# Two more y buffers and a longer lookahead in the second stage of a four-layer convolution kernel

## The chip, the cores and the metric

The kernel runs on one core of one Trainium2 chip. The metric is the time on the device in microseconds (us), the median of three runs. The profile is that of one further execution of the same program.

## What is computed

The input is `x` of shape [8192, 8, 16, 16] in float32: 8192 samples of 8 channels and 16 x 16 points. Four layers follow each other, each of the form x + f(gn(x)), where `gn` is a normalization over the two channels of each of four groups:

```python
x = x + L0(gn(x))   # a tensor-train operator with three cores of rank 8, plus a bias
x = x + L1(gn(x))   # 3x3 convolution, then batch norm over all samples, then relu
x = x + L2(gn(x))   # input and weights quantized to +-127 by their maxima, 3x3 convolution
x = x + L3(gn(x))   # weights binarized to sign * mean, 3x3 convolution with edge padding
```

with, for the two layers that cut the kernel into stages,

```python
# L1: the mean and variance go over all 8192 samples
mean = y.mean(axis=(0, 2, 3), keepdims=True)
var = y.var(axis=(0, 2, 3), keepdims=True)
return relu(gamma * (y - mean) * rsqrt(var + EPS) + beta)
# L2: the scale needs the largest value of the whole normalized input
sx = MAX_Q / jnp.max(jnp.abs(x))
```

The mean and variance of layer 1 need all samples before one can be finished, and so does the maximum of layer 2. That is why the kernel goes over the data three times.

## The kernel before, in words

**Tiles.** The samples are cut into `NT` = 64 tiles of 128. A tile has 128 partitions (8 channels x 16 rows) and 2,048 float32 values in each (128 samples x 16 columns), 1 MiB in all. Tiles that don't fit into SBUF between the stages are kept in DRAM: `x1_d` (the sum after layer 0), `y_d` (the convolution of layer 1), `x2_d` (the centred sum after layer 1).

**Stage 1** (lines 328 to 685) works in quarters of a tile, 256 steps. It computes layer 0 on TensorE, adds it to x, normalizes, computes the convolution of layer 1 and its statistics. Each x1 and y goes to DRAM, except for the last `STAY` = 4 tiles, which remain in SBUF. Layer 0 needs its operand in another arrangement: `limbs` (line 401, its stores are line 409) writes a high and a low part of it to `limb_d` in DRAM by 8 small transfers on SyncE's queue (SP), and `fetch` (line 411) reads it back into one of two `xl` buffers by a transfer that GpSimd issues, 252 in all. The descriptors of such a transfer are written by GpSimd into a reserve in SBUF. The buffers `sq0` and `sq1` serve for squares there, `xh` for the high parts of the limbs; TensorE's expanded operands lie in `u`.

**Constants** (lines 688 to 708): mean and variance of layer 1 become the pair `bn_a`, `bn_b`.

**Stage 2** (lines 743 to 871) is the one that the change touches. It goes over the tiles in `order2`: the four that stayed first, then 0 to 59. In the following, "tile i" is the i-th in this order. Its steps for one tile are

- `sum2`: ScalarE applies relu(bn_a y + bn_b) to the y buffer, GpSimd adds it to the x buffer, so that the y buffer is free from here on,
- `square2` (ScalarE), `sums2` (TensorE, sums of groups), `stats2` and `sigma2` (VectorE, ScalarE and a pow on GpSimd: mean and 1/deviation),
- `spread2`: VectorE builds `diag_b` from them and transposes it, TensorE spreads it to all partitions (`gb`, `gr`),
- `centre2`: VectorE subtracts the mean from x in two halves, and SP stores x to `x2_d` (line 827). The last 13 tiles before the last five (`KEEP` = 13, `LATE` = 5) are not stored but kept for stage 3,
- `range2`: VectorE takes maxima for the scale of layer 2 into `top`.

The loop (line 853) runs over i and calls in turn: the loads, `sum2(i)`, `sums2(i-2)`, `spread2(i-3)`, `square2(i-1)`, `stats2(i-2)`, `centre2(i-3)`, `sigma2(i-2)`, `range2(i-3)`. Work on TensorE, VectorE, ScalarE and GpSimd is kept in this order (`InOrder`, lines 31 to 44; line 43 is what the profile shows for all of it). SP's transfers are ordered by the framework, which may put them in another order than the code's.

**Buffers of stage 2.** There are 13 x buffers (`x_slots`, line 95, and two `xk` of line 746) and 8 y buffers (`y_slots`, line 96: one of the tiles that stayed, `sq0`, `sq1`, `xh`; and four `yk` of line 747). `load2(i)` (line 104, its transfer is line 111) loads tile i's y into y buffer (i - 4 + 1) mod 8 and its x into x buffer i mod 13. So the x of tile j takes the place of tile j - 13, which must have been stored, and the y of tile j that of tile j - 8, whose `sum2` must be done.

```python
AHEAD2 = len(y_slots) - 1
```

`AHEAD2` (line 845), 7 here, is the lookahead: step i of the loop loads y, then x of tile i + 7, and the store of tile i - 3 comes later in that step. The first loads are earlier: those of tiles 4 to 6 stand in the code at the end of stage 1 (lines 663 to 677: y and x of 4 and 5 in the last but one step, x of 6 and 7, then y of 6), the y of 7 and both of 8 and 9 ahead of the loop, those of 10 at step 1. The last five tiles (`LATE`, lines 858 to 861) are loaded one transfer a step into y buffers that have become free.

**Stage 3** (from line 888 on) computes layers 2 and 3. The order of its steps is that of a table of due times (`PHASE`, `PERIOD`). It loads x from `x2_d` (line 911) into the same x buffers, uses `sq0`, `sq1`, `xh` and `y_stay[3]` as work space, and stores the output (line 1053).

Of the kernel before, what the change touches and what calls it, by code (L numbers as in the profile page):

```python
# [8 lines left out]
F32 = mybir.dt.float32  # L9
# [9 lines left out]
P = 128  # L19
C, H, W = 8, 16, 16  # L20
CH = C * H
F = P * W
G = 4
R = 8
NQ = 4
# [37 lines left out]
def tile_net(ctx: ExitStack, tc: tile.TileContext, xb, xt_in, pack0, pack1, pack2, out):  # L63
    nc = tc.nc
    NT = xt_in.shape[0]
# [10 lines left out]
    def load_pack(src, parts, t):  # L76
        nc.scalar.dma_start(t, src)
        views, at = {}, 0
        for key, n in parts:
# [3 lines left out]


    hold = ctx.enter_context(tc.tile_pool(name="hold", bufs=1))
    xs, bs, ys, sqs, (xh,) = ([hold.tile([P, F], F32, name=f"{n}{k}") for k in range(m)]
                            for n, m in (("xs", 4), ("bs", 2), ("ys", 2), ("sq", 2), ("xh", 1)))
    us = [hold.tile([P, 2 * F], F32, name=f"u{k}") for k in range(2)]

    STAY = 4  # L90
    order2 = list(range(NT - STAY, NT)) + list(range(NT - STAY))
    y_stay = [ys[NT % 2], ys[(NT - 1) % 2], bs[NT % 2], bs[(NT - 1) % 2]]
    y_of = dict(zip(order2, y_stay))

    x_slots = ([xs[t % 4] for t in order2[:STAY]] + [u[:, h * F:(h + 1) * F] for u in us for h in range(2)] + y_stay[:3])
    y_slots = [y_stay[3]] + sqs + [xh]
    T2 = [dict() for _ in range(NT)]

    LATE = 5 if NT >= KEEP + STAY + 3 else 0
# [4 lines left out]
    def load2(i, what="yx"):  # L104
        for k in what:
            if k == "x":
                T2[i]["x"] = x_slots[i % KEEP]
            else:
                T2[i]["y"] = y_stay[i] if i < STAY else y_slots[(i - STAY + 1) % len(y_slots)]
            if i >= STAY:  # L110
                nc.sync.dma_start(T2[i][k], (x1_d if k == "x" else y_d)[order2[i]])
# [216 lines left out]
    with first as s:  # L328
# [19 lines left out]
        def load_b(t):  # L348
            T[t]["xb"] = bs[t % 2]
            n = F // 2 if t == 0 else F  # L350
            for a in range(0, F, n):
                nc.sync.dma_start(T[t]["xb"][:, a:a + n], xb[t][:, a:a + n])
# [84 lines left out]
        def main(t, q, between, n0=None):  # L437
            u = T[t].pop(("u", q)).rearrange("p b (s n) -> p b s n", s=R)
            po = ps_m.tile([P, BANK], F32, name=f"po_{t}_{q}", tag="mm")
            parts = [(0, QS)] if n0 is None else [(0, n0), (n0, QS)]  # L440
            for a, b in parts:
                for r in range(R):
                    for f, args in between.get(r, ()) if b == QS else ():
                        f(*args)
                    pe.matmul(samples(po)[:, a:b], core01[:, r], u[:, a:b, r, :], start=(r == 0), stop=(r == R - 1))
            cols = slice(q * BANK, (q + 1) * BANK)
            x = T[t]["x"]
            dve.tensor_tensor(x[:, cols], po, x[:, cols], ALU.add)
# [66 lines left out]
        def conv1(t, q):  # L515
            v = T[t].pop(("v", q))
            pm, po = (ps_m.tile([P, k, NC], F32, name=f"{n}_{t}_{q}", tag="mm") for n, k in (("pm", 4), ("pc", 2)))
            for ps, at in ((pm, 0), (po, 4)):
                for k in range(ps.shape[1]):
                    pe.matmul(ps[:, k], L["fast1"][:, at + k], v[:, at + k], start=True, stop=True)  # L520
            m = wk.tile([P, 2, NC], F32, name=f"m_{t}_{q}", tag="m")
            act.activation(m[:, 0], pm[:, 0], AF.Identity, bias=L["b1"], scale=1.0)
            act.copy(m[:, 1], pm[:, 2])
            T[t]["m", q] = m, pm, po
# [40 lines left out]
        def quarter_of(n, lag):  # L565

            t, q = divmod(n - lag, NQ)
            return (t, q) if 0 <= t < NT else None
# [34 lines left out]
        for n in range(NT * NQ):  # L603
            t, q = divmod(n, NQ)
            steps = {}

            def at(r, ok, f, *args):
                if ok:
                    steps.setdefault(r, []).append((f, args))

            def at1(r, f, lag):
                if quarter_of(n, lag):
                    at(r, True, f, *quarter_of(n, lag))

            last, before, ahead = t == NT - 1, t > 0, t + 2 < NT
            if n > 0:
                next(rest, None)
                if n == 1:
                    next(rest, None)
            tn, qn = divmod(n + 1, NQ)  # L620
            at(0, tn < NT, expand, tn, qn, 0)
            at(4, tn < NT, expand, tn, qn, 1)
            at1(0, conv1_input, LAG)
            if n < NT * NQ - 1:
                at1(6, conv1_scaled, LAG - 1)
            if n == 0 and NT > 1:
                at(1, True, norm_b_spread, 1)
                at(1, True, norm_b_apply, 1)
                at(1, True, add_bias, 1)
            if q == 0:  # L630
                if before and t - 1 not in y_of:
                    nc.sync.dma_start(x1_d[t - 1], T[t - 1]["x"])
                at(1, before, norm_sums, t - 1)
                at(4, before, norm_stats, t - 1)
                if ahead:
                    load_b(t + 2)
            elif q == 1:
                at(1, ahead, norm_b_square, t + 2)
                at(1, before, norm_apply, t - 1)
                at(4, t + 3 < NT, load_t, t + 3)  # L640
            elif q == 2:
                at(1, ahead, norm_b_sums, t + 2)
                at(1, ahead, norm_b_stats, t + 2)
            else:
                at(1, before and t + 3 < NT, add_bias, t + 3)
                at(1, ahead, norm_b_spread, t + 2)
                at(1, ahead, norm_b_apply, t + 2)
            at1(3, conv1_output, LAG + 1)

            for m in {0: [], 1: [4, 5], 2: [6, 7], 3: []}.get(n, [n + NQ]):  # L650
                at(0 if n < 3 else 2, m < NT * NQ, limbs, *divmod(m, NQ))
            for m in {0: [], 1: [4, 5], 2: []}.get(n, [n + 3]):
                at(5, m < NT * NQ, fetch, *divmod(m, NQ))

            at(2, n == NQ and NT > 2, add_bias, 2)
            at(5, n == NQ + 1 and NT > 3, add_bias, 3)
            if last:
                at(2, q > 1, quarter_apply, t, q - 2)
                at(2, q > 0, quarter_stats, t, q - 1)
            main(t, q, steps, n0=QS // 2 if n == 0 else None)  # L660
            if quarter_of(n, LAG):
                conv1(*quarter_of(n, LAG))
            if n == NT * NQ - 2 and NT > STAY + 3:
                load2(STAY)
                load2(STAY + 1)

        t = NT - 1
        if NT > STAY + 3:
            load2(STAY + 2, "x")
            load2(STAY + 3, "x")  # L670
        conv1_output(t - 1, 1)
# [1 line left out]
        quarter_stats(t, 3)  # L673
        conv1_direct(t, 0)
        quarter_apply(t, 2)
        if NT > STAY + 3:
            load2(STAY + 2, "y")
        conv1_direct(t, 1)
        for q in (2, 3):
            conv1_direct(t - 1, q)  # L680
# [63 lines left out]
    with tc.tile_pool(name="p2", bufs=2) as p2, tc.tile_pool(name="ps2", bufs=2, space=PSUM) as ps2:  # L744
# [9 lines left out]
        for k in range(3):  # L754
            nc.tensor.matmul(kps, L["gpad"].rearrange("p q j -> p (q j)"), L["band3"][:, k],
                             start=(k == 0), stop=(k == 2))
        ksum = p2.tile([P, CH], F32, name="ksum", tag="ksum", bufs=1)
        nc.vector.tensor_tensor(ksum.rearrange("p (c h) -> p c h", c=C), kps.rearrange("p (c h) -> p c h", c=C),
                                L["mean3"].unsqueeze(2).to_broadcast([P, C, H]), ALU.mult)
        nc.vector.tensor_tensor(L["corr"], L["corr"], ksum, ALU.subtract)  # L760
# [79 lines left out]
        def on(i, f):  # L840
            if 0 <= i < NT:
                f(i)

        BEGUN = STAY + 3 if NT > STAY + 3 else STAY
        AHEAD2 = len(y_slots) - 1


        free = STAY + AHEAD2 - 1
        for i in [*range(STAY), *range(BEGUN, free)]:
            on(i, lambda i: load2(i, "y" if i == BEGUN > STAY else "yx"))  # L850
        y_used = {}
        late = [(k, j) for j in range(NT - LATE, NT) for k in "yx"]
        for i in range(NT + 4):
            if i == 1:
                on(free, load2)
            if i + AHEAD2 < NT - LATE:
                on(i + AHEAD2, lambda i: i <= free or load2(i))
            elif late:
                k, j = late.pop(0)
                T2[j][k] = y_used[i - 1]  # L860
                nc.sync.dma_start(T2[j][k], (x1_d if k == "x" else y_d)[order2[j]])
            if i == 8:
                operands3()
            on(i, sum2)
            on(i - 2, sums2)
            on(i - 3, spread2)
            on(i - 1, square2)
            on(i - 2, stats2)
            on(i - 3, centre2)
            on(i - 2, sigma2)  # L870
            on(i - 3, range2)
# [276 lines left out]
```

## Time and profile before

| | |
|---|---|
| three runs | 3,817.96, 3,817.99, 3,819.87 us; median 3,817.99 |
| the profiled execution | 3,817.41 us, of which its span (first to last instruction) 3,815.6 |
| granted TensorE clock | 0.96 |
| instructions | 54,624 |
| busy, of the span | PE (TensorE matmul) 94%, DVE (VectorE) 88%, POOL (GpSimd) 79%, ACT (ScalarE) 66% |
| DMA | 961.06 MB, mean 252 GB/s |
| stage 1 | 0 to 2,621 us: PE busy 2,601.7, DVE 2,311.4, POOL 1,968.3, DMA share 0.78 |
| stage 2 | 2,627.7 to 3,058 us: PE busy 256.9, DVE 395.1, POOL 359.4, DMA share 0.94 |
| stage 3 | 3,062 to 3,815 us: PE busy 729.6, DVE 652.1, POOL 687.2, DMA share 0.42 |

How to read the profile. It has a page with the busy time of each engine, then 40 slices of the span, each of 95.4 us. In a slice a digit is a busy share in tenths; GB/s is what the DMA engines moved. Groups of instructions have the form "engine, operation, output<-input, count". "Waits" lists for each engine and group the idle time in front of it, after the name of what ended that idle time: total in us, count, longest. The timeline gives for each instruction its start (us from the span's start), its duration, its engine and its line; SPq is SyncE issuing a transfer, so the duration there is not that of the transfer. "To landing" is the time from issue until the data are there. The chain of waits goes back from the last instruction: at each step to what released it.

### The profile page before, as it was taken

How to read it: one execution, taken by the hardware profiler on the slowest of the kernel's cores; microseconds unless marked ns; L12 is line 12 of the kernel's file. 1: busy time of each engine (PE TensorE's matmuls, PEld its weight loads, DVE VectorE, ACT ScalarE, POOL GpSimd, SP SyncE). 2: the span in 40 equal slices, each digit the busy share in tenths (PEclk: the TensorE clock that was granted, in tenths of full speed). 3: DMA queues.
4: the chain of work that ended last, by engine and by line, in shares of the span. 5: the costliest groups of instructions: out<-in, count | busy, mean ns of one | idle time of the engine just before them, and what ended most of it. 6: DMA issues, size and time to landing. Idle time of an engine off the chain costs nothing.

```text
span 3815.6 us, 54624 instructions
## 1 busy us (share of the span) xinstructions
PE 3590.2 (94%) x17286; PEld 2137.8 (56%) x17350; DVE 3364.9 (88%) x6020; ACT 2524.9 (66%) x2741; POOL 3015.9 (79%) x3102
## 2 busy tenths in 40 slices
PE   8999999999999999999999999997566579999999
PEld 4666666666666666666666666663122146666665
DVE  8988888888888888888888888877999888888887
ACT  5666666666666666666666666665665578888885
POOL 4877777778777777777787777765888869999998
PEclk9999999999999999999999999998776689999999
DMA  5787787887877878878788888766999824444442
GB/s 213 252 271 256 258 271 254 262 262 253 271 253 262 273 255 258 269 252 264 260 256 269 254 264 268 252 195 248 421 426 426 337 86 184 188 181 188 188 166 111
DMA packets 210816, 961.06 MB, mean 252 GB/s; under 512 B 44896, under 2 KB 45152, under 8 KB 110048
## 3 DMA queue, kind: packets, MB, share of 16 engines
q1 hardware_dynamic: 173808, 692.22, 49.0%
q0 software_dynamic: 36288, 264.26, 23.5%
q8 instruction: 139, 2.28, 0.2%
q14 instruction: 149, 1.22, 0.1%
q10 hardware_dynamic: 432, 1.08, 0.1%
HBM read 578.84 MB, written 378.54 MB: 251 GB/s over the span
## 4 chain that ended last, share of the span: by engine, by line
PE 86%; DVE 6%; DMA 5%; issue 1%; POOL 1%; ACT 1%; SPq 0%; DVEq 0%; POOLq 0%; ACTq 0%
PE po L43 45%; PE pu L43 12%; PE pf L43 10%; PE pm L43 6%; PE pq L43 4%; PE pc L43 3%; PE s L43 3%; DVE top L43 2%; DMA u<-x_d 1%; DMA sq<-y_d 1%; PE ps_a L43 1%; DMA ys<-x_d 1%; DMA x_d<-u 1%; DMA x_d<-ys 1%; DMA x_d<-xs 1%
## 5 line engine op out<-in xcount | busy, mean ns | idle before, releaser
L43 PE MATMUL po<-u,core 128*128 128x512 f32 (+1 forms) x4112 | 1844.8, 591 | 0.0
L43 ACT COPY u<-pu 128x2048 f32<-128x2048 f32 x512 | 956.4, 1868 | 513.2 <-PE pu L43 513.2
L43 PEld LDWEIGHTS po<-u,core 128*128 128x128 f32 x4112 | 744.8, 190 | 737.2 <-issue 736.2
L43 PE MATMUL pu<-core2r,xl 128*128 128x256 f32 x4032 | 678.5, 310 | 4.5 <-ACT u L43 3.7
L43 PEld LDWEIGHTS pu<-core2r,xl 128*128 128x128 f32 x4032 | 527.9, 189 | 127.7 <-issue 122.9
L43 POOL TENSOR_TENSOR bs<-bs,xh 128x512 fp32r<-128x512 f32 (+1 forms) x253 | 325.7, 1288 | 201.4 <-ACT xh L43 201.4
L43 POOL TENSOR_TENSOR v<-e 128x128 f32<-128x128 f32 x750 | 397.2, 541 | 0.0
L43 DVE TENSOR_TENSOR xs<-po,xs 128x512 f32<-128x512 f32 x256 | 177.0, 691 | 219.4 <-PE po L43 219.1
L43 ACT ACTIVATE m<-pm,b 128x128 f32<-128x128 f32 x250 | 91.9, 368 | 396.0 <-PE pm L43 396.0
L43 PEld LDWEIGHTS pm<-v,fast 128*128 128x128 f32 x2000 | 262.5, 191 | 119.7 <-issue 106.4
L43 POOL TENSOR_TENSOR e<-x1n,x 128x512 f32<-128x512 f32 x250 | 306.1, 1225 | 21.6 <-ACT x L43 13.8
L43 DVE TENSOR_TENSOR bs<-bs,stat 128x1024 f32<-128x1024 f32 x252 | 290.6, 1215 | 2.1
L43 POOL TENSOR_TENSOR xs<-xs,w 128x2048 f32<-128x2048 f32 x64 | 291.4, 4553 | 0.6 <-DMA xs<-in_xt 0.6
L43 PE MATMUL pm<-v,fast 128*128 128x128 f32 x2000 | 263.5, 275 | 0.0
L43 ACT ACTIVATE x<-x1n 128x512 f32<-128x512 f32 x500 | 247.0, 544 | 7.6 <-DVE x1n L43 7.6
L43 PE MATMUL pf<-hi,sign 128*128 128x512 f32 x768 | 231.6, 439 | 0.1
L43 POOL DMA_DIRECT2D xl<-limb_d x252 | 149.8, 594 | 102.5 <-ACT x L43 28.6
L43 PE MATMUL pf<-lo,sign 128*128 128x512 f32 x768 | 218.9, 422 | 0.0
L43 POOL TENSOR_TENSOR v<-r 128x128 f32<-128x128 f32 x500 | 215.6, 448 | 0.0
L43 ACT ACTIVATE sq<-xs 128x2048 f32<-128x2048 f32 x103 | 197.4, 1916 | 4.8 <-POOL xs L43 4.6
L43 PE MATMUL pq<-q,band 128*128 128x480 bf16 (+1 forms) x704 | 188.3, 387 | 10.1 <-ACT q L43 6.4
L43 PE MATMUL gb<-rows_c,sel 128*128 128x128 f32 x128 | 41.3, 417 | 165.7 <-DVE rows_c L43 165.7
(322 smaller groups left out, 7102.7 us busy)
## 6 DMA issues: line engine op xcount, KB each, us to landing
xl<-limb_d POOLq DMA_DIRECT2D x252, 1024.0 KB, 7.4
x_d<-xs SPq DMA_DIRECT2D x76, 1024.0 KB, 8.4
xs<-in_xt SPq DMA_DIRECT2D x64, 1024.0 KB, 7.6
bs<-in_xb SPq DMA_DIRECT2D x63, 1024.0 KB, 5.7
limb_d<-xh SPq DMA_DIRECT2D x1008, 64.0 KB, 4.4
limb_d<-bs SPq DMA_DIRECT2D x1008, 64.0 KB, 5.2
y_d<-ys SPq DMA_DIRECT2D x60, 1024.0 KB, 8.0
u<-x_d SPq DMA_DIRECT2D x34, 1024.0 KB, 6.0
```

The costliest lines, as they stand in the source:

```text
L43: return self.tc.keep_in_program_order(op(*args, **kwargs))
```

## The change

In stage 2 there are two more y buffers, `ex0` and `ex1` (128 x 2,048 float32 each, 8,192 bytes a partition), so 10 in place of 8. `AHEAD2` becomes 9. The 13 x buffers stay as they are. The space comes from GpSimd's reserve for descriptors, which is set to 1,536 bytes (before: not set, the default), and from `ksum`, a small tile of its own that now lies in a `top` buffer.

The order of `y_slots` is now `y_stay[3]`, `ex0`, `ex1`, `sq0`, `sq1`, `xh`, `yk0` to `yk3`. The y of tiles 4 and 5 goes to `ex0` and `ex1`, that of 6 and 7 to `sq0` and `sq1`, that of 8 to `xh`.

The loads at the end of stage 1 stand at other places: the y of 4 and 5 four steps earlier (step 250 of 256), then at step 254 y of 6, x of 4, y of 7, x of 5; x of 6 and 7 as before; and y of 8 where y of 6 had been. Ahead of the loop stand x of 8, y and x of 9, and y of 10, 11 and 12. The x of 10, 11 and 12 are loaded at steps 1, 2 and 3 of the loop. From step 4 on, step i loads y, then x of tile i + 9. The late loads begin two steps earlier.

```diff
     xs, bs, ys, sqs, (xh,), ex = ([hold.tile([P, F], F32, name=f"{n}{k}") for k in range(m)]
-                            for n, m in (("xs", 4), ("bs", 2), ("ys", 2), ("sq", 2), ("xh", 1)))
+                            for n, m in (("xs", 4), ("bs", 2), ("ys", 2), ("sq", 2), ("xh", 1), ("ex", 2)))
...
-    y_slots = [y_stay[3]] + sqs + [xh]
+    y_slots = [y_stay[3]] + ex + sqs + [xh]
...
-            if n == NT * NQ - 2 and NT > STAY + 3:
-                load2(STAY)
-                load2(STAY + 1)
+            if NT > STAY + 5:
+                for i, k in {NT * NQ - 6: [(0, "y"), (1, "y")], NT * NQ - 2: [(2, "y"), (0, "x"), (3, "y"), (1, "x")]}.get(n, []):
+                    load2(STAY + i, k)
...
-        if NT > STAY + 3:
-            load2(STAY + 2, "y")
+        if NT > STAY + 5:
+            load2(STAY + 4, "y")
...
-        ksum = p2.tile([P, CH], F32, name="ksum", tag="ksum", bufs=1)
+        ksum = p2.tile([P, 4, P], F32, name="ksum", tag="top")[:, 0]
...
-        BEGUN = STAY + 3 if NT > STAY + 3 else STAY
         AHEAD2 = len(y_slots) - 1
-        free = STAY + AHEAD2 - 1
-        for i in [*range(STAY), *range(BEGUN, free)]:
-            on(i, lambda i: load2(i, "y" if i == BEGUN > STAY else "yx"))
+        begun = NT > STAY + 5
+        for i in range(STAY):
+            load2(i)
+        for i in range(STAY, min(NT - LATE, STAY + AHEAD2)):
+            if i >= STAY + 5 or not begun:
+                load2(i, "y")
+            if (i >= STAY + 4 or not begun) and i < STAY + 6:
+                load2(i, "x")
...
-            if i == 1:
-                on(free, load2)
+            if 1 <= i <= 3:
+                on(STAY + 5 + i, lambda i: load2(i, "x"))
             if i + AHEAD2 < NT - LATE:
-                on(i + AHEAD2, lambda i: i <= free or load2(i))
+                on(i + AHEAD2, lambda i: i < STAY + AHEAD2 or load2(i))
...
-    nc = bacc.Bacc("TRN2", target_bir_lowering=False, num_devices=1)
+    nc = bacc.Bacc("TRN2", target_bir_lowering=False, num_devices=1, dynamic_dma_scratch_size=1536)
```

More of the change, by code (lines that the diff above doesn't have):

```diff
@@ L85, in tile_net @@
     hold = ctx.enter_context(tc.tile_pool(name="hold", bufs=1))
-    xs, bs, ys, sqs, (xh,) = ([hold.tile([P, F], F32, name=f"{n}{k}") for k in range(m)]
-                            for n, m in (("xs", 4), ("bs", 2), ("ys", 2), ("sq", 2), ("xh", 1)))
+    xs, bs, ys, sqs, (xh,), ex = ([hold.tile([P, F], F32, name=f"{n}{k}") for k in range(m)]
+                            for n, m in (("xs", 4), ("bs", 2), ("ys", 2), ("sq", 2), ("xh", 1), ("ex", 2)))
     us = [hold.tile([P, 2 * F], F32, name=f"u{k}") for k in range(2)]
@@ L675, in tile_net @@
         quarter_apply(t, 2)
-        if NT > STAY + 3:
-            load2(STAY + 2, "y")
+        if NT > STAY + 5:
+            load2(STAY + 4, "y")
         conv1_direct(t, 1)
```

## The prediction

> **What bounds the kernel now.** I read the page first, slices of the span before groups, because the change touches one stage only. Slices 29 to 33 are the second stage (2,628 to 3,058 us).
>
> ```profile
> PE   8999999999999999999999999997566579999999
> DVE  8988888888888888888888888877999888888887
> DMA  5787787887877878878788888766999824444442
> GB/s 213 252 271 256 258 271 254 262 262 253 271 253 262 273 255 258 269 252 264 260 256 269 254 264 268 252 195 248 421 426 426 337 86 184 188 181 188 188 166 111
> ```
>
> TensorE is full before and after the stage and half empty in it; DVE and DMA are both full there. Which of the two sets the end? The busy times by stretch (columns: us, PE, PEld, DVE, ACT, POOL, clock, DMA share, GB/s):
>
> ```profile
> 2860.00:2920.00 60.00, 36.04 (x188) 12.84 (x192) 58.36 (x92) 37.33 (x39) 52.08 (x20) 0.70 1.01 426
> 2920.00:2992.00 72.00, 43.44 (x198) 13.22 (x191) 62.42 (x96) 38.25 (x38) 53.01 (x20) 0.64 1.01 427
> ```
>
> Until about tile 45 DVE is the bound (58.4 of 60 us, one tile in some 6.3 us), although the transfers are slower: a tile is two loads and a store, 3 x 2.45 us = 7.4 us. The kernel lives on tiles loaded ahead. From 2,930 us that stock is used up. The waits of 2,900 to 3,010 us name what it costs:
>
> ```profile
> ACT yk L43 <- DMA yk<-y_d: 21.0, 7, 4.1
> DVE diag_b L43 <- POOL gnst L43: 8.9, 7, 1.6
> ```
>
> DVE waits for GpSimd's pow, which stands behind the x + y add of a tile whose x has just landed. So **8.9 us** is all that better loading can give back in this stage; the end is DVE-bound again.
>
> How the loads are issued is seen in SyncE's own timeline, at the start of the stage and later:
>
> ```profile
> 2645.99 0.32 SPq L827 DMA_DIRECT2D x_d<-xs  x1
> 2646.69 0.32 SPq L111 DMA_DIRECT2D bs<-y_d  x1
> 2647.07 1.22 SPq L111 DMA_DIRECT2D ys<-x_d  x1
> ...
> 2738.24 0.32 SPq L827 DMA_DIRECT2D x_d<-xs  x1
> 2740.69 0.32 SPq L111 DMA_DIRECT2D yk<-y_d  x1
> 2743.16 0.32 SPq L111 DMA_DIRECT2D bs<-x_d  x1
> ```
>
> Later the queue issues one transfer every 2.45 us, and the chain of waits says why: each waits for the one issued eight earlier (19.6 = 8 x 2.45).
>
> ```profile
> 2841.58 19.61 DMA x_d<-xs
> 2861.26 19.59 DMA xs<-x_d
> ```
>
> **The skill.** "DMA: Bandwidth & Descriptors", section "Anatomy of one DMA": a DMA's semaphore wait is done by the issuing sequencer before dispatch, the DMA engines wait for nothing. So a waiting load holds up all behind it on SP. The trace agrees: near the stage's end a load sits 4.7 us until a store of 2,960.27 us (19.9 us to landing) is in, and the y load behind it goes 0.4 us after it:
>
> ```profile
> 2975.20 0.32 SPq L111 DMA_DIRECT2D yk<-y_d  x1
> 2980.21 0.32 SPq L111 DMA_DIRECT2D u<-x_d  x1
> 2980.59 0.47 SPq L111 DMA_DIRECT2D yk<-y_d  x1
> ```
>
> Same page, "Two DMAs through the same engine are not ordered": a transfer that needs an earlier one finished must wait for its semaphore; queue order is not enough. Hence a load into a stored slot waits for the store's landing. In stage 3 the trace shows this pair bare: store 3,116.22, landing 3.9 us later (page of DMA issues), load 3,120.16.
>
> For the reserve: "SBUF — State Buffer", "SBUF size", gives 16 KiB a partition to GpSimd's descriptor ring; "DMA: Bandwidth & Descriptors", "The descriptor swizzle", 9 descriptors an engine for 1 MiB, of 16 B each. The trace agrees with the 9: 36,288 packets / 252 fetches / 16 engines.
>
> ```profile
> q0 software_dynamic: 36288, 264.26, 23.5%
> xl<-limb_d POOLq DMA_DIRECT2D x252, 1024.0 KB, 7.4
> ```
>
> **The reserve.** My estimate from these sections: 16,384 B hold 113 fetches, 1,536 B hold 96 descriptors, 10 fetches. Two xl buffers allow two in flight, each landed after 7.4 us, one issued each 10 us. The 114th and 228th fetch, which must already reuse a slot, took 0.62 us like others. Cost 0. Were it to wait each time, GpSimd, 77% busy in stage 1, has 2.3 us a step to hide it.
>
> **ksum in a top buffer** moves one small tile: 0.
>
> **Loads in stage 1.** y of tiles 4 and 5 go to the new buffers, which nothing else uses; tiles 6 and 7 take the places in sq that 4 and 5 had, tile 8 takes xh. That is 2 MiB more, 4.9 us of transfers, while the DMA share of 2,560 to 2,600 us is 0.37, so 25 us lie idle. Without that cover a limb fetch would land some 5 us later, once: at most 5 us.
>
> **Prologue.** Six loads at 2,621 to 2,627 us as before, but the first is now tile 8's x, which waited until 2,625.58 (for bn_b), where two y loads had gone at 2,621.62. Then x of 10, 11 and 12 at steps 1 to 3, where 11 and 12 had stood at steps 4 and 5. Nine loads from 2,625.6: the first lands after 4.7, the last at 2,625.6 + 4.7 + 8 x 2.45 = 2,650. Tile 0's store, issued at 2,646.0, then lands at 2,652.4 instead of 2,650.7: **1.7 us later, with two more tiles (4 MiB) in**.
>
> **The loop.** Now step i loads tile i+9 instead of i+7, but there are still 13 x buffers. Tile j's x goes where tile j-13 was. Before, from that store to this load are 8 transfers, just the depth of the queue. Now tile j-13 is stored in step j-10 and the load is in step j-9: two transfers later. SP waits for the store to land, and behind it stand the next store and the next y load; the next store is what the next x load waits for. The queue cannot be eight deep any more: it falls to one or two when a store lands and rises to four.
>
> What it gains: up to tile 56 (the last that DVE waits for) the old order has 3 x 46 = 138 transfers from tile 0's store on, the new one 3 x 44 = 132, since stores run two tiles nearer to their slots. 6 x 2.45 - 1.7 = **13.0 us earlier**, of which DVE can use 8.9.
>
> What it costs: the loss b per tile from a shallow queue. Not shown in the steady trace, so bounds. Below: none, since one y (2.45 us) is still moving when the store lands; then the gain stays. Above: tile 8's x load, issued with one transfer ahead, landed 2,632.7, 3.9 us after the one before (2,628.8), so 1.4 us lost. Nearest row: the start of the stage, with 2 to 6 in the queue. Landings by window: tile 0's store 2,645.99 + 4.7 = 2,650.7; eleven transfers later 2,664.59 + 15.3 = 2,679.9. 29.2 - 11 x 2.45 = 2.2 us over 3.67 tiles, **b = 0.60**. I take this: it is the only stretch in which loads and stores mix in a short queue. Tiles 13 to 56 are 44: 44 x 0.60 = 26.4; 26.4 - 13.0 = **+13.4 us** for tile 56's x. DVE is already waiting there, so the end moves by the same. The profiled execution took 3,817.4 (span 3,815.6), against a median of 3,818.0: 3,817.4 + 13.4 = 3,831, beside the median the same.
>
> What is late next: the last five tiles' loads need no stores (2 x 2.45 = 4.9 us a tile against DVE's 5.8), so DVE is the bound again, and stage 3 starts from there.
>
> **Rivals.** (1) Likeliest, as above, **3,831**, chance 0.50, own range 3,824 to 3,858: needs b over 0.45. (2) The **lead wins**, 3,818 - 8.9 = **3,809**, chance 0.22: a stock two tiles deeper and one transfer always in flight cover the hand-over; decides for it if b is under (13.0 - 8.9) / 44 = 0.1. For it: from 2,700 us on 426 GB/s without a gap; against: those stretches have the full queue. (3) **Balance**, **3,818**, chance 0.26: b near 13.0 / 44 = 0.3. SP's order is not the code's: this y load for stage 2 stands in the code after limb stores of later steps, yet went first:
>
> ```profile
> 2515.02 0.47 SPq L111 DMA_DIRECT2D sq<-y_d  x1
> 2518.66 1.77 SPq L409 DMA_DIRECT2D limb_d<-xh  x4
> ```
>
> So the x load may be put behind the next store; then two transfers, 4.9 us, are in flight at each hand-over, not one, and b halves. (4) The ring stalls GpSimd, or the change does not do what it says: 0.02; at 5 us a fetch, over 1,000 us slower.
>
> **Numbers.** 0.2% is 7.6 us, about what a measurement of this kernel can tell from no change. Faster is case 2 less its part with a gain under 7.6: 0.20; same is case 3 and that part: 0.29; slower, cases 1 and 4: 0.51. With b from 0 to 1.4 the times run from 3,809 to 3,818 + 61.6 - 13.0 = 3,867; the range keeps the lower end, gives up the ring and the top of case 1: 3,808 to 3,855.
>
> **What would show it.** Right: in SP's timeline, x loads of stage 2 issued 0.1 us after a store's landing, stores landing in 6 to 11 us instead of 19.6, DMA under 426 GB/s from 2,660 to 3,000 us, and DVE waiting for pow well before 2,930 us and for more than 8.9 us. Case 2: these waits gone at 426 GB/s. Case 3: the next store ahead of the x load. GpSimd's fetches unchanged at 0.6 us, or case 4. It is wrong if transfers stay dense in a queue two to four deep.

## The result and the profile after

The changed kernel takes **4,000.78 us** (median of four runs, 3,999.54 to 4,001.24) against 3,818.55 us for the kernel before on the same chip (3,817.96 to 3,819.87). The ratio is 1.0478, interval 1.0466 to 1.049: 182 us slower, where 13 had been predicted. The profiled execution has a span of 3,997.7 us, 182.1 more than before.

The slices of the page of the changed kernel show where it went. Slices here are 99.9 us long, so the second stage is slices 27 to 32.

```profile
PE   8999999999999999999999999965333359999999
DVE  8988888888888888888888888778555588888987
...
DMA  5887787878878787878787887577777724444442
GB/s 205 277 265 265 257 264 260 261 264 257 268 252 273 249 272 249 266 258 271 255 265 259 265 253 255 167 291 266 269 266 268 282 107 190 185 184 188 181 169 116
```

Ahead of the stage and behind it the busy times are as before. In it, DVE is busy half of the time and DMA moves some 267 GB/s where it moved 426. Neither is full: something waits. The stretches of the changed kernel (us, PE, PEld, DVE, ACT, POOL, clock, DMA share, GB/s) say the same with numbers:

```profile
2760.00:2860.00 100.00, 43.60 (x200) 14.03 (x200) 63.73 (x97) 36.49 (x38) 50.30 (x19) 0.64 0.79 275
2860.00:3000.00 140.00, 54.36 (x240) 17.68 (x240) 73.70 (x112) 48.17 (x48) 63.98 (x24) 0.60 0.77 264
```

From 2,860 us on the DMA engines are busy 0.77 of the time (before 1.01), and while busy they move 264 / 0.77 = 343 GB/s (before 426 / 1.01 = 422). So there are both gaps and slower packets.

The wait that the prediction watched, in the second stage of the changed kernel, has gone from 12.2 us (8.9 of them late in the stage) to

```profile
DVE diag_b L43 <- POOL gnst L43: 189.6, 37, 5.9
```

and SyncE's own waits in that stage give the reason. All 46 x loads that go into a stored slot (tiles 13 to 58) waited for the store's landing, some 10.3 us each, 473 us in sum:

```profile
SPq L111 <- DMA x_d<-xs: 157.9, 16, 10.8
SPq L111 <- DMA x_d<-u: 156.8, 15, 10.7
SPq L111 <- DMA x_d<-xk: 63.5, 6, 10.6
SPq L111 <- DMA x_d<-ys: 63.2, 6, 10.9
SPq L111 <- DMA x_d<-bs: 31.6, 3, 10.7
```

SyncE's timeline of the changed kernel shows the rhythm: x load, next store, next y load within one microsecond, then nothing for nine to eleven.

```profile
2652.45 0.32 SPq L111 DMA_DIRECT2D xs<-x_d  x1
2652.86 0.38 SPq L827 DMA_DIRECT2D x_d<-xs  x1
2653.34 0.41 SPq L111 DMA_DIRECT2D ex<-y_d  x1
2662.79 0.32 SPq L111 DMA_DIRECT2D xs<-x_d  x1
...
3170.08 0.32 SPq L111 DMA_DIRECT2D u<-x_d  x1
3170.49 0.38 SPq L827 DMA_DIRECT2D x_d<-u  x1
3170.96 0.38 SPq L111 DMA_DIRECT2D xh<-y_d  x1
3181.97 0.32 SPq L111 DMA_DIRECT2D u<-x_d  x1
```

The first x load of this kind is at 2,652.45 us, the last at 3,181.97: 45 cycles of **11.77 us**, where three transfers at full rate take 7.36. The chain of waits of the changed kernel (start, length; shorter steps in between are left out) runs from store to store:

```profile
2803.36 11.17 DMA x_d<-xs
2814.54 0.03 SPq L111
2814.60 0.32 SPq L111
2815.01 11.65 DMA x_d<-xs
2826.68 0.03 SPq L111
2826.74 0.32 SPq L111
2827.17 11.27 DMA x_d<-xs
```

The first store shown lands 11.2 us after its issue; 0.07 us later the x load is issued, 0.4 us after it the next store; and so on. Each store waits for the x load ahead of it in SyncE's queue, and that for the store before.

### The profile page after: what moved, and what is told of

It reads as the page before. It is cut to its first block, busy times and chain, and to the rows that moved or that the text cites. A ratio compares the mean times of both kernels' runs of the same rounds, so it can differ in the third digit from the quotient of the medians.

```text
span 3997.7 us, 54626 instructions
## 1 busy us (share of the span) xinstructions
PE 3600.8 (90%) x17286; PEld 2142.3 (54%) x17350; DVE 3369.8 (84%) x6020; ACT 2525.1 (63%) x2741; POOL 3015.1 (75%) x3102
## 4 chain that ended last, share of the span: by engine, by line
PE 81%; DMA 11%; DVE 5%; issue 1%; POOL 1%; ACT 1%; SPq 0%; DVEq 0%; POOLq 0%
PE po L43 43%; PE pu L43 12%; PE pf L43 10%; PE pm L43 6%; PE pq L43 4%; DMA x_d<-xs 3%; DMA x_d<-u 3%; PE pc L43 3%; PE s L43 3%; DVE top L43 2%; DMA x_d<-ys 1%; DMA x_d<-xk 1%; DMA x_d<-bs 1%; PE ps_a L43 1%; PE pd L43 0%
## 5 line engine op out<-in xcount | busy, mean ns | idle before, releaser
L43 PEld LDWEIGHTS gb<-rows_c,sel 128*128 128x128 f32 x128 | 29.0, 282 | 422.0 <-issue 411.7
```

Of the source, the lines that this page charges most:

```text
L43: return self.tc.keep_in_program_order(op(*args, **kwargs))
```

## The experiments

Ratios are to runs of the kernel before on the same chip, with a 95% interval. "Distance" is how many transfers later on SyncE's queue the x load comes after the store of the tile whose place it takes: 8 before, 2 after the change (store, y load, x load).

| kernel | distance | time, us | ratio |
|---|---|---|---|
| reserve alone | 8 | 3,817.85 | 0.9999 (0.9991 to 1.0008) |
| changed, x 7 ahead | 8 | 3,817.50 | 0.9997 (0.9989 to 1.0005) |
| before, x 9 ahead | 2 | 4,009.34 | 1.0482 (1.0453 to 1.0511) |
| changed, x 8 ahead | 5 | 3,810.27 | 0.9980 (0.9971 to 0.9989) |
| changed, x load ahead of y load | 1 | 3,997.87 | 1.0472 (1.0458 to 1.0487) |
| changed, x load behind the next store | 4 | 3,808.96 | 0.9976 (0.9967 to 0.9984) |
| 15 x and 8 y buffers | 8 | 3,812.94 | 0.9986 (0.9979 to 0.9992) |
| stores on ScalarE, behind the loads | - | 3,939.39 | 1.0318 (1.0301 to 1.0336) |
| stores on ScalarE, ahead of the loads | - | 3,847.43 | 1.0080 (1.0066 to 1.0094) |
| before, x 9 ahead, behind the next store | 4 | 3,818.28 | 1.0002 (0.9994 to 1.0010) |
| store and x load alone | 1 | 3,888.52 | 1.0186 (1.0169 to 1.0203) |

**The reserve alone.**

```diff
-    nc = bacc.Bacc("TRN2", target_bir_lowering=False, num_devices=1)
+    nc = bacc.Bacc("TRN2", target_bir_lowering=False, num_devices=1, dynamic_dma_scratch_size=1536)
```

> The kernel before with GpSimd's reserve set to 1,536 bytes and nothing else. Hand-over theory (each x load waits at the head of SyncE's queue for a store issued two transfers earlier): the reserve has no part in it, 3,818 us, within 3 us of before, fetches still 0.6 us each. Reserve theory (ten slots instead of 113 make GpSimd or its transfers wait): the loss shows here, in stage 1, from a few us to the whole 180.

Measured 3,817.85 us. The fetches, by the tile they write (shortest, median, longest in ns), are as in the changed kernel, where the median is 599:

```profile
L43 POOL DMA_DIRECT2D xl<-limb_d x252: 567/600/859, 42.8 to 2576.4; - x126
```

The reserve has no part in the loss.

**The lookahead of x.** Three kernels that vary the distance: the changed kernel with x 7 ahead (or 8, with 8 in place of 7 in the lines shown), and the kernel before with x 9 ahead:

```diff
-            if i + AHEAD2 < NT - LATE:
-                on(i + AHEAD2, lambda i: i < STAY + AHEAD2 or load2(i))
-            elif late:
+            if STAY <= i < NT - LATE - AHEAD2:
+                load2(i + AHEAD2, "y")
+            if KEEP <= i + 7 < NT - LATE:
+                load2(i + 7, "x")
+            elif late and i + 7 >= NT - LATE:
```

```diff
+            if 2 <= i <= 3:
+                load2(i + AHEAD2 + 2, "x")
             if i + AHEAD2 < NT - LATE:
-                on(i + AHEAD2, lambda i: i <= free or load2(i))
+                on(i + AHEAD2, lambda i: i <= free or load2(i, "y"))
+                if KEEP <= i + AHEAD2 + 2 < NT - LATE:
+                    load2(i + AHEAD2 + 2, "x")
```

> The changed kernel with x loaded 7 tiles ahead as before (y stays 9 ahead, ten y buffers, small reserve, new places of the first loads). Hand-over theory: from a store to the load that waits for it are 8 transfers again, the queue is full, all of the loss goes: 3,808 to 3,818 us, 426 GB/s from 2,700 to 2,900 us. Of the 8.9 us that VectorE waited before, some 3 to 5 may be won, since two more y tiles are in at the stage's start. Buffer theory (ten y buffers and y loads 9 ahead make the transfers slower): stays near 4,000 us.

> The kernel before with x loaded 9 tiles ahead (8 y buffers 7 ahead, reserve and first loads as before, x of tiles 11 and 12 two steps earlier). Hand-over theory: a store and its load are two transfers apart, so a period of some 11.9 us a tile as in the changed kernel, 44 tiles x (11.85 - 7.36) = 198 us less a lead of some 10: 3,995 to 4,015 us. Buffer or reserve theory: no loss, 3,818 us.

> The changed kernel with x loaded 8 tiles ahead: five transfers from a store to the load that waits for it. Hand-over theory: two tiles pass per hand-over. The store issued right behind a released load has about five transfers ahead: [...] just hidden, 3,808 to 3,822 us. If the restart's slow packets come at each hand-over whatever is in flight, 2 us a tile stay: some 3,890 us. Theory that the loss grows in proportion to the lookahead: half of it, some 3,905 us.

The kernel before with nothing but a longer lookahead of x loses as much as the whole change (4,009 us in its three timed runs, 3,980.5 in its profiled one). The changed kernel with the old distance of 8 loses nothing. So neither the buffers nor the first loads cost anything that can be seen; the distance does. (In it the late loads begin where they did before the change; the kernel with x behind the next store, below, has them two steps earlier and loses nothing.) At a distance of 5 the loss is gone altogether, not halved: it does not go in proportion to the lookahead. In the kernel with x 8 ahead the transfers are dense again, and it is 7.7 us faster than before:

```profile
2760.00:2860.00 100.00, 62.11 (x320) 20.32 (x320) 97.52 (x152) 63.39 (x64) 87.50 (x32) 0.73 1.01 426
```

The few us hoped for from x 7 ahead did not come. Its waits of 2,900 to 3,010 us name x; the waits for y of the kernel before (21.0 us for the `yk` buffers) are gone, and VectorE waits as long as it did, because an x is late instead:

```profile
DVE diag_b L43 <- POOL gnst L43: 8.7, 7, 1.6
POOL xs L43 <- DMA xs<-x_d: 3.9, 2, 1.9
POOL ys L43 <- DMA ys<-x_d: 3.8, 2, 1.9
```

**The place of the x load in the queue.** The lookahead of 9 stays. First with the x load directly behind its store, and SyncE's queue kept in the order of the code; then behind the next store:

```diff
+        queue2[0] = InOrder(tc, nc.sync)
...
-                on(i + AHEAD2, lambda i: i < STAY + AHEAD2 or load2(i))
+                on(i + AHEAD2, lambda i: i < STAY + AHEAD2 or load2(i, "xy"))
```

```diff
-                on(i + AHEAD2, lambda i: i < STAY + AHEAD2 or load2(i))
+                on(i + AHEAD2, lambda i: i < STAY + AHEAD2 or load2(i, "y"))
...
             on(i - 3, centre2)
+            if KEEP <= i + AHEAD2 < NT - LATE:
+                load2(i + AHEAD2, "x")
```

> The changed kernel with the x load of tile i + 9 ahead of its y load, and SyncE's queue in stage 2 kept as written: store, the x load that waits for it, y load. Same transfers, same lookahead. Hand-over theory: a period is 7.36 us of transfers plus what of a hand-over of L us is not covered by the transfers queued between the store and its load, 2.45 us each. The changed kernel has one (y) and loses 4.5, so L = 6.9; here there is none: 14.3 us a tile, 44 x 6.9 - 13 = 291 us over before, some 4,110 us. Rival (the slow packets after a restart set the period, whatever the order): as the changed kernel, 4,000 us.

> The changed kernel with the x load of tile i + 9 placed behind the store of tile i - 3 instead of ahead of it: four transfers from a store to its load, and the next store no longer stands behind the waiting load. Lookahead unchanged. Hand-over theory: three transfers cover 7.35 of 6.9 us, no loss, and the lead is won: 3,808 to 3,815 us. Lookahead theory (x 9 tiles ahead with 13 x buffers is itself what costs): near 4,000 us.

The first missed: not 4,110 but 3,997.87 us, the rival's number. A y load between store and x load does not shorten the cycle, because it has not landed when x and the next store are issued, and stands ahead of them: in the changed kernel the y load of 2,827.63 us lands after 13.2 us, 1.6 us behind the issue of the next store (2,839.25). In both orders two transfers lie ahead of the next store. Little of y is left by then: from 2,837.5 to 2,839.5 us the DMA share is 0.07 and 29 GB/s move, about what one of the 16 DMA engines moves at full rate (426 / 16 = 27). Nearly all of the engines stand idle; that the next landings are held up by this small rest is argued from the order of the landings. SyncE's timeline of the kernel with x ahead of y shows cycles of (2,826.82 - 2,803.84) / 2 = 11.5 us here, and of 11.6 over 22 cycles (x loads at 2,700.13 and 2,955.78 us):

```profile
2803.84 0.32 SPq L43 DMA_DIRECT2D xs<-x_d  x1
2804.21 0.42 SPq L43 DMA_DIRECT2D sq<-y_d  x1
2804.73 0.38 SPq L43 DMA_DIRECT2D x_d<-xs  x1
...
2826.82 0.32 SPq L43 DMA_DIRECT2D xs<-x_d  x1
```

The second gave 3,808.96 us: the same lookahead and the same transfers as the changed kernel, the x load moved past one store, and 192 us less; 9 us faster than the kernel before. Its forecast came from the same sum that missed for the first kernel, so the hit does not speak for that sum, only against the theory that the lookahead itself costs. Its x loads still wait for stores at the head of the queue, over 5 us each (SyncE's waits in the stage), but nothing is lost by it, since the next store has been issued already:

```profile
SPq L111 <- DMA x_d<-u: 75.3, 14, 6.5
SPq L111 <- DMA x_d<-xs: 75.0, 14, 6.2
...
SPq L111 <- DMA x_d<-ys: 35.3, 6, 5.9
SPq L111 <- DMA x_d<-xk: 34.6, 6, 6.0
```

```profile
2860.00:3000.00 140.00, 89.19 (x448) 29.01 (x440) 136.31 (x211) 89.37 (x90) 122.37 (x45) 0.69 1.01 425
```

VectorE is busy 136.3 of 140 us there; its wait for the pow is down to one of 3.3 us. This version beats both kernels.

**Fifteen x buffers.** The two new buffers go to x (the edit is against the changed kernel; the first loads, not shown here, go nearly back to their old places).

```diff
-KEEP = 13
+KEEP = 15
...
+            if 4 <= i < NT - LATE - 7:
+                load2(i + 7, "y")
+            if KEEP <= i + 9 < NT - LATE:
+                load2(i + 9, "x")
```

> The kernel before with the two new buffers given to x instead of y: 15 x buffers, x 9 and y 7 tiles ahead, 15 tiles kept for stage 3 instead of 13, so two stores and two loads fewer; small reserve. Hand-over theory: eight transfers from a store to its load, queue full, some 13 us of lead, VectorE never waits: about 9 us less than before, 3,806 to 3,811 us. Rival: x is not what is late, 3,815 to 3,818 us.

Measured 3,812.94 us, between the two. Of 2,900 to 3,010 us this kernel's waits name y:

```profile
ACT yk L43 <- DMA yk<-y_d: 12.3, 6, 3.4
ACT sq L43 <- DMA sq<-y_d: 6.9, 2, 3.4
DVE diag_b L43 <- POOL gnst L43: 4.8, 4, 1.3
```

**The stores on ScalarE's queue.** Two kernels, which tell whether the waiting load hurts by itself or because a store stands behind it. In the first the store is written one step later, behind the load that takes the same place; so what it stores is the next tile's x from before the layer, and it waits for that load. In the second it stands at the start of the step, ahead of the load.

```diff
-                nc.sync.dma_start(x2_d[order2[i]], x)
+                T[i]["store"] = x
...
+        def store2(i):
+            if "store" in T[i]:
+                act.dma_start(x2_d[order2[i]], T[i].pop("store"))
```

The call stands behind the loads in the first kernel, and ahead of them in the second:

```diff
             on(i - 2, stats2)
+            on(i - 4, store2)
             on(i - 3, centre2)
```

```diff
         for i in range(NT + 4):
+            on(i - 4, store2)
             if 1 <= i <= 3:
```

> The changed kernel with the stores of stage 2 issued by ScalarE's queue, one step later, so that no store stands behind a waiting load; all else unchanged, the x load of tile j still waits for the store of tile j - 13. Hand-over theory: a store no longer waits for the load ahead of it, the chain from store to store is cut, the waits on SyncE overlap with transfers of y: 3,808 to 3,820 us. Rival (a load that waits at the head of SyncE's queue costs by itself, whatever stands behind it): near 4,000 us.

> The changed kernel with the stores of stage 2 issued by ScalarE, at the start of the next step and thus ahead of the load that takes the same place. The x load of tile i + 9 still waits at the head of SyncE's queue for the store of tile i - 4, with the y load behind it, but no store waits for a load. If the loss is the chain in which the next store stands behind the waiting load: 3,808 to 3,820 us. If a load waiting at the head of SyncE's queue, with few transfers in flight, is enough: near 4,000 us.

The first is no test of the question, since it turns the wait round: the store waits for the load, and ScalarE with it (3,939.39 us). The second answers half. Its transfers are dense, so the chain is cut, though SyncE's waits name a store at the head of its queue 41 times, 5.7 us each:

```profile
2700.00:2860.00 160.00, 91.86 (x456) 27.31 (x448) 139.94 (x212) 88.43 (x88) 122.43 (x45) 0.69 1.01 426
```

Yet it is 30 us slower than the kernel before. ScalarE's timeline of that kernel shows its queue standing for 2 to 4 us ahead of each store (the columns in brackets are the idle time before and what ended it):

```profile
2813.11 0.17 ACT L43 ACTIVATE sq_c<-psc 128x4 f32<-128x4 f32 x1
2817.20 0.33 ACTq L43 DMA_DIRECT2D x_d<-ys  x1
2817.57 2.10 ACT L43 ACTIVATE xh<-xh,bn_b,bn_a 128x2048 f32<-128x2048 f32 x1 [4.29 <-DVE rows_c L43]
...
2823.63 0.33 ACTq L43 DMA_DIRECT2D x_d<-bs  x1
2824.01 2.09 ACT L43 ACTIVATE yk<-yk,bn_b,bn_a 128x2048 f32<-128x2048 f32 x1 [2.42 <-DMA ex<-y_d]
```

The waits of the two stores shown end with the landing of a y load that SyncE had issued: that of 2,797.77 us landed at 2,817.17, the store went out at 2,817.20; that of 2,805.14 landed at 2,823.54, the store went out at 2,823.63. Each of these loads is the eighth transfer before the store in the order of the code, on whichever queue, just as each transfer of the kernel before waited for the eighth before it. From tile 14 on the stage runs at 7.4 us a tile, the pace of the transfers, instead of VectorE's 6.3: the stock of tiles loaded ahead is of no use to an engine that must wait for a recent load. That these waits of ScalarE make up the whole 30 us is argued, not tested by a run of its own.

**Are the buffers needed?** The kernel before, x 9 ahead and behind the next store, with 8 y buffers:

```diff
+            if 2 <= i <= 3:
+                load2(i + AHEAD2 + 2, "x")
...
-                on(i + AHEAD2, lambda i: i <= free or load2(i))
+                on(i + AHEAD2, lambda i: i <= free or load2(i, "y"))
...
             on(i - 3, centre2)
+            if KEEP <= i + AHEAD2 + 2 < NT - LATE:
+                load2(i + AHEAD2 + 2, "x")
```

> The kernel before with x loaded 9 tiles ahead, each x load behind the store of its step (four transfers from a store to its load), y 7 ahead, 8 y buffers, the reserve as before. If the lead of the x loads alone is what VectorE's waits lacked: 3,808 to 3,813 us without the two buffers. If the y loads need the same lead: 3,815 to 3,818 us. If 13 x buffers and a lead of 9 cost by themselves: 3,980 us or more, as with the x load ahead of the store.

Measured 3,818.28 us, no gain. The waits in its stage name y:

```profile
ACT yk L43 <- DMA yk<-y_d: 22.0, 7, 3.9
DVE diag_b L43 <- POOL gnst L43: 11.9, 9, 3.3
```

Together with the kernel of x 7 ahead: with 13 x buffers, y alone further ahead gains nothing (x is late), x alone nothing (y is late), both together 7.7 to 9.3 us. The kernel with fifteen x buffers also has y 7 ahead and still gained 5 us; but there two stores and two loads fall away, of which the stores are 2 x 2.45 = 4.9 us of this stage's transfers, and the first loads differ. Which of these gave the 5 us was not separated.

**What a cycle is made of.** The kernel with x directly behind its store, without the y loads of tiles 13 to 58:

```diff
-                on(i + AHEAD2, lambda i: i < STAY + AHEAD2 or load2(i, "xy"))
+                on(i + AHEAD2, lambda i: i < STAY + AHEAD2 or (T2[i].update(y=y_slots[(i - STAY + 1) % len(y_slots)]), load2(i, "x")))
```

> Store and x load alone: the changed kernel with the x load directly behind the store that it waits for, and the y loads of tiles 13 to 58 left out (their y buffers hold older data, so the output is not the reference's). It leaves out 46 of the 3 x 46 transfers of the stretch. A cycle is then one load and one store, each waiting for the other: estimate 0.5 us of issue + 2.45 + the 3.86 of a store by itself + the slow packets after a restart. If a y load costs a full-rate 2.45 us of the cycle of 11.6, the cycle is 9.2 us, VectorE (6.3 us a tile) runs out of tiles, and the time is some 3,885 us, slower than the kernel before with a third more transfers. If it costs 3.9, as y lands behind x there, the cycle is 7.8 us and the time some 3,825 us. If the number of bytes set the time: 4.9 us a tile, hidden behind VectorE, 3,808 us.

Measured 3,888.52 us, the 9.2 us case. From SyncE's timeline the stores are at

```profile
2706.56 0.39 SPq L43 DMA_DIRECT2D x_d<-u  x1
...
2957.48 0.38 SPq L43 DMA_DIRECT2D x_d<-xk  x1
```

which is 27 cycles of 9.29 us. A third of the transfers of the stretch is gone, and the kernel is 1.9% slower than before. So the time is not set by the number of bytes. Its terms: 0.5 us of issue, the load ahead 2.45, a store by itself 3.86 (stage 3 of the kernel before), together 6.8; 2.5 are left. With the y load it is 0.5 + 2 x 2.45 + 3.86 = 9.3, and 11.6 (x ahead of y) and 11.8 (the changed kernel) were measured: 2.3 and 2.5 left. The remainder is much the same with and without y; what makes it is not shown.

## Why the prediction was wrong

**What bounds the kernel: right.** VectorE waits some 9 us late in the stage, and that is all that better loading can give: the two best kernels gave 7.7 and 9.3 us.

**Reserve, ksum, loads in stage 1: right**, as far as it shows. The reserve alone is at 0.9999. With the old distance, all other parts of the change but the earlier late loads are together at 0.9997. That 1,536 bytes hold ten fetches stays an estimate: the runs show only that nothing was lost. (The 16 B of a descriptor, which it uses, stand in the section "Terms" of the Trainium skill's "DMA: Bandwidth & Descriptors", not in the one that the prediction names.)

**Prologue: right in what it gave.** Tile 0's store was to land at 2,652.4 us; the x load that waits for it was issued at 2,652.45. The way there was not quite as described: a y load went first, at 2,622.34 us, ahead of tile 8's x, and the store was issued 0.5 us later than before.

**The mechanism of the loop: right.** x loads go out 0.07 us after a store's landing, stores land in some 11.3 us instead of 19.6 (the prediction had 6 to 11), the transfers fall under 426 GB/s, VectorE waits for the pow all through.

**The size of b: wrong, and this is the failed step.** It was put at 0.60 us a tile, with 0 and 1.4 as bounds. Measured is 11.77 - 7.36 = 4.41. With it the prediction's own sum gives 44 x 4.41 - 13.0 = 181 us, and 182 were measured. So close a match is in part luck: tile 56's x landed at 3,167.5 us instead of 2,992.5, 175 us later and not 181, and the last x that VectorE waited for is now tile 58's. These differences are small beside the error in b. The 0.60 came from the start of the stage, called the only stretch in which loads and stores mix in a short queue. But there a store is issued as soon as VectorE has the tile, so stores never stand behind a waiting load. The feature that decides, a store behind a load behind a store, is in no row of the kernel before. The upper bound of 1.4 came from two loads, and had no store in it.

Part of it could have been reckoned from lines that the prediction quoted. From one store to the next in the new order: issue 0.5, two transfers ahead 2 x 2.45, a bare store 3.9; 9.3 us against 7.36, which puts b at 1.9 and the loss at 44 x 1.9 - 13 = 71 us. This estimate counts y in full. The lower bound of 0 rested on "one y is still moving when the store lands". That y covers the hand-over, but lies ahead of the next store as well, so it pays nothing; the kernels with x ahead of y (11.6 us a cycle) and without y (9.29) show it, no row of before does. Nor does any row of before show the other 2.5 us of b.

**The rivals.** Case 2 had the gain and its time, 3,809, but not all that it needs: besides the deeper stock, the next store issued ahead of the waiting x load. Case 3 guessed that this order would halve b; it removes it, and SyncE's queue did not take it by itself (x load, store, y load, as the code has it). Case 4, the ring, did not happen.

**What stays open.** The 2.5 us that the sum of latencies leaves are a remainder, not explained. What the stretches divide is the whole 4.4 us of b: 2.8 are gap (a DMA share of 0.77 is 0.24 x 11.8 = 2.8 us of a cycle against 1.01) and 1.6 slower packets ((0.77 / 1.01) x 11.8 - 7.36). The word "restart" of the expectations is not enough for the slow packets: in one cycle of the kernel with x ahead of y, 426 GB/s moved from 2,817.5 to 2,820.0 us, soon after the pause, then 239 from 2,820.5 to 2,823.0, and 418 from 2,823.5 to 2,825.5. Why packets are slower there was not tried. Of the kernel before with x 9 ahead, the one execution with a trace was 29 us faster than the others; its cycles are 11.11 us (24 from 2,692.78 to 2,959.51), and 44 x (11.77 - 11.11) is 29. Why they are shorter is open.

## What to carry to other kernels

When a load reuses a buffer that a store must empty first, count the transfers between the two on their queue, and ask whether the *next* store stands behind the waiting load. If so, as here, the queue runs in cycles of one store's latency with all that lies ahead of it (11.8 us, where the transfers at full rate take 7.36). Work such a cycle out as a sum of latencies, not as a loss from full rate, and take the sum as too low: here it gave 9.3. Prefetching further with the same number of buffers shortens that distance: move the load behind the next store, or look ahead a little less, and give both operands of a tile more lead, not one alone.

## What was not expected of the hardware

- A chain of one 1 MiB store and one 1 MiB load, each waiting for the other, runs at 9.29 us a pair, 227 GB/s (store and x load alone), where the full queue of the kernel before moves 426.
- Adding a third transfer to such a chain costs about the 2.45 us that it takes in a full queue (9.29 to 11.6 and 11.8), whether it stands ahead of the load or behind it.
- A distance of 4 was enough for the full rate (425 GB/s), though the load waits some 5 us at the head of the queue each time; at 2 it was 264 in the changed kernel. The step between was not tried.
- With the stores on ScalarE's queue, ScalarE waited at both stores looked at for a load that SyncE had issued, the eighth transfer before the store in the code; the kernel took 30 us more than the kernel before, at a DMA rate of 426 GB/s.
- At the hand-over looked at in the changed kernel (2,837.5 to 2,839.5 us) a y load had not landed, yet only 29 GB/s moved, at a DMA share of 0.07: as much as one engine of 16.
